# A Mamba stage whose scans carry a trailing column, with the norm root as a power, the residual summed by TensorE, fourteen products with C on GpSimd and a new order of issue

## The chip, the cores and the metric

The kernel runs on one core of one Trainium2 chip. The metric is device time in microseconds (us) of one execution. Shown are three timed executions and one that the hardware profiler recorded.

## The reference, cut to what matters

The program computes a window attention layer, a positional convolution, six Mamba layers, a gated feed-forward layer, a causal pooling and a mixture of experts over images of 2 x 256 x 56 x 56. The change touches the Mamba layers alone. There are B = 2 images of S = 3136 tokens, 512 inner channels and 16 states for each.

```python
def step(h, inp):
    u_t, dt_t, B_t, C_t = inp
    h = jnp.exp(dt_t[..., None] * A) * h + (dt_t * u_t)[..., None] * B_t[:, None, :]
    y_t = jnp.einsum('bds,bs->bd', h, C_t)
    return (h, y_t)
...
dt = jax.nn.softplus(dt_r @ dt_w + dt_b)
A = -jnp.exp(A_log)
y = selective_scan(uc, dt, A, Bm, Cm, Dp)
y = y * jax.nn.silu(z)
return y @ out_w
```

Each of the six layers works on an RMS-normed copy of the tokens, x * rsqrt(mean(x * x) + 1e-5), and adds its result to the running sum (the residual). A layernorm stands ahead of the first layer, an RMS norm behind the last.

## The kernel before, in words

`conv_phase` (attention and positions), `mamba_phase` and `tail_phase` (the rest) follow one another. `mamba_phase` cuts an image into 7 chunks of T = 448 tokens; 2 images x 6 layers x 7 chunks make 84 chunks. In a chunk the inner state has 512 x 16 rows of 448 tokens. 128 rows stand on the partitions, two such rows side by side make one step, and `order` (line 777) lists the 32 steps of a chunk: 4 blocks k of 128 channels, 4 groups ng of states, 2 pairs pr.

A step i has these parts:
- `decays(i)` (L799): two exp activations on ScalarE write exp(dt * A) for both rows into `da` (PSUM, three buffers). A first column ahead of each row comes from a BIG value in `dtr`, so that its decay is 0 there and the scan of the second row starts afresh.
- `inputs(i)` (L815, L816): ScalarE copies the two carried states into the first column of each row of `x` (SBUF, nine buffers), and GpSimd multiplies dt*u by B into the rest.
- `scan(i)` (L836): VectorE scans both rows in one instruction, h = da * h + x, and writes over `da`, or over `x` for the steps in `on_pool` (line 780, 12 of 32).
- the product with C (`times_c`, L829): on VectorE directly after the scan, or on GpSimd as `pool_product` for the steps in `on_pool`. It writes `x`.
- `keep(i)` (L825): ScalarE copies the last column of each row to `state`, for the next chunk of the same layer.
- `gather(i)` (L846, L851), for every second step: TensorE sums the products over states into `acc`. `gate(i)` (L861), for every eighth, multiplies by silu(z) on VectorE.

Beside the steps, each chunk prepares the next one: `project` (L554), the convolution (L572), `x_project`, `x_keep` (its B and C rows go through DRAM into `bc`, spread over the partitions), `dt_project`, `dt_keep`, `dt_softplus` (L636), `dt_out` (GpSimd forms dt*u, L644; dt and dt*u go to DRAM, L642, L646) and `repeat` (L773), which brings them back spread over the partitions with 8 DMAs of SP's queue a block: `dt_back` for block 0, `fetch` for the others. `y_project` (L700) and `y_add` (L707, VectorE) add the layer's result to the residual `res`. The norm ahead of a layer is `n_squares` (L654, L658), `n_root` (sqrt on ScalarE, L665), `n_invert` (reciprocal on VectorE, L668), `n_spread` (L674, TensorE) and `n_weighted` (L682, VectorE). All matmul results but `acc` pass through one PSUM buffer, `mm`.

Three tables set the order. `places` gives each preparing part its place in a chunk, counted in steps; `first` places the input layernorm's parts (in five chunks of the first layer, and in the seven of the second for the other image); `last` the final norm's. The parts of the steps stand at fixed distances from their step (lines 928 to 939). All are sorted by place (line 961) and issued in that order; each engine then works its own queue in order and waits on semaphores. `load` brings a layer's weights (L507 to L515); `w_in` has one buffer.

Of the kernel before, what the change touches and what calls it, by code (L numbers as in the profile page):

```python
# [10 lines left out]
F32 = mybir.dt.float32  # L11
# [442 lines left out]
def mamba_phase(ctx: ExitStack, tc: tile.TileContext, I, t1_d, t2_d):  # L454
# [9 lines left out]
    ctx.enter_context(tc.manual_schedule())  # L464
    T = MT
    cp = ctx.enter_context(tc.tile_pool(name="mb_const", bufs=1))
# [12 lines left out]
    nc.vector.memset(mean_w, 1.0 / C)  # L479
    eps = ones_column(nc, cp, 1e-5, "mb_eps")  # L480
    sum_w = cp.tile([P, HD], F32, name="sum_w")
    nc.sync.dma_start(sum_w, I["sum_w"])
# [4 lines left out]
    res = cp.tile([P, 2, S], F32, name="res")  # L487
    dtrs = [cp.tile([P, 4, T + 1], F32, name=f"dtr{n}") for n in range(2)]
    for t in dtrs:
        nc.gpsimd.memset(t[:, :, 0:1], BIG)  # L490

    r1_d = [dp.tile([P, 2, T], F32, name=f"r1_d{c}", bufs=1) for c in range(MCH)]

    def wide(t, n=2):
        return t.unsqueeze(1).to_broadcast([P, n, T])

# [112 lines left out]
    def x_keep(j):  # L609

        xd = M["xd"] = one.tile([DTR + 2 * DS, T], F32, name="xd")
        nc.scalar.copy(xd, M["mm"])  # L612
        bc_d = dp.tile([2 * DS, T], F32, name="bc_d")
        nc.sync.dma_start(bc_d, xd[DTR:, :])
        bc = QS[j + 1]["bc"] = two.tile([P, 8, T + 4], F32, name="bc")[:, :, 3 : T + 3]
        for n in range(4):
            nc.sync.dma_start(
                bc[chunk(n, HD)],
                bc_d.rearrange("(m n) t -> n m t", n=4)[n].unsqueeze(0).to_broadcast([HD, 8, T]),
            )  # L620
        QS[j + 1]["dt_d"], QS[j + 1]["dtu_d"] = {}, {}
# [41 lines left out]
    def root(key):  # L663
        rs = M[key] = one.tile([MTG, ng], F32, name="rs" + key)
        nc.scalar.activation(rs, M["mm"][:MTG, :ng], AF.Sqrt, bias=eps[:MTG])  # L665

    def invert(key):
        nc.vector.reciprocal(M[key], M[key])  # L668

# [26 lines left out]
    def y_project(j, k):  # L696

        ps = M["mm"] = mm()[:, :T]
        for d in range(NB):
            nc.tensor.matmul(  # L700
                ps, lhsT=layer_of(j - 1)["w_out"][:, d, chunk(k, P)],
                rhs=QS[j - 1]["hz"][:, d, :], start=(d == 0), stop=(d == NB - 1),
            )

    def y_add(j, k):
        rc = residual(j - 1)
        nc.vector.tensor_tensor(rc[:, k, :], rc[:, k, :], M["mm"], ALU.add)  # L707

# [58 lines left out]
    def repeat(Q, k):  # L767

        dtr = dtrs[k % 2]
        dtur = two.tile([P, 4, T + 4], F32, name="dtur")[:, :, 1 : T + 1]  # L770
        for t, src in ((dtr[:, :, 1:], Q["dt_d"]), (dtur, Q["dtu_d"])):
            for n in range(4):
                nc.sync.dma_start(t[chunk(n, HD)], src[k].rearrange("(g p) t -> p g t", p=HD))  # L773
        Q[k] = dtr, dtur
# [4 lines left out]

    on_pool = (2, 3, 5, 7, 8, 9, 10, 15, 19, 21, 22, 26)  # L780
    chunks = [(b, layer, c) for b in range(B) for layer in range(NL) for c in range(MCH)]
# [9 lines left out]
    def decays(i):  # L791
# [3 lines left out]
        da = pda.tile([P, 1024], F32, name="da")  # L795
        D[i] = da[:, : 2 * (T + 1)]
        for g in range(2):
            col = (4 * k + 2 * pr + g) * 4 + ng
            nc.scalar.activation(  # L799
                D[i][:, chunk(g, T + 1)], dtr[:, 2 * pr + g, :], AF.Exp,  # L800
                scale=L["am"][:, col : col + 1],
            )
# [6 lines left out]
    def inputs(i):  # L809

        j, s, k, ng, pr = at(i)
        Q = QS[j]
        X[i] = xp.tile([P, 2 * (T + 1)], F32, name="x")
        x = both(X[i])
# [8 lines left out]
    def keep(i):  # L823
        h = X[i] if i % ns in on_pool else D[i]
        nc.scalar.copy(states(i), both(h)[:, :, T : T + 1])  # L825

    def times_c(i, engine, h):
        j, s, k, ng, pr = at(i)
        engine.tensor_tensor(  # L829
            both(X[i])[:, :, 1:], both(h)[:, :, 1:], wide(QS[j]["bc"][:, 4 + ng, :]), ALU.mult  # L830
        )

    def scan(i):

        h = X[i] if i % ns in on_pool else D[i]
        nc.vector.tensor_tensor_scan(h, D[i], X[i], 0.0, ALU.mult, ALU.add)  # L836
        if i % ns not in on_pool:
            times_c(i, nc.vector, h)

    def gather(i):  # L840
# [9 lines left out]
        for g in range(4):  # L850
            nc.tensor.matmul(  # L851
                acc[0][chunk(g, HD), :T], lhsT=sum_w, rhs=both(X[i - 1 + g // 2])[:, g % 2, 1:],
                start=False, stop=(ng == 3), tile_position=(0, HD * g),
# [8 lines left out]

    def pool_product(i):
        times_c(i, nc.gpsimd, X[i])

# [17 lines left out]
    def load_rest(j):  # L883
# [5 lines left out]
    places = {  # L889
        (u_project, 0): 1.304, (u_keep, 0): 2.607, (z_project, 0): 3.501, (z_keep, 0): 3.952,  # L890
        (u_project, 1): 4.609, (u_keep, 1): 5.234, (y_project, 1): 6.869, (y_add, 1): 7.331,
        (y_project, 0): 7.461, (y_add, 0): 9.223, (u_convolve, 0): 10.048, (u_add, 0): 10.687,
        (u_project, 2): 10.964, (u_keep, 2): 11.995, (u_convolve, 1): 12.277, (u_add, 1): 13.134,
        (u_convolve, 2): 14.792, (u_add, 2): 15.184, (u_project, 3): 15.393, (u_keep, 3): 16.616,
        (u_convolve, 3): 17.440, (u_add, 3): 17.991, (z_project, 1): 18.040, (u_silu,): 18.479,
        (z_keep, 1): 18.732, (x_project,): 19.334, (x_keep,): 20.167, (dt_project, 2): 20.825,
        (dt_keep, 2): 21.601, (dt_project, 0): 21.808, (dt_keep, 0): 22.204,
        (dt_project, 1): 23.295, (dt_keep, 1): 23.374, (dt_project, 3): 24.269,
        (dt_keep, 3): 24.913, (dt_softplus,): 24.942, (dt_out, 0): 25.013, (dt_back,): 25.337,
        (z_project, 2): 25.840, (dt_out, 1): 26.057, (z_keep, 2): 26.747, (z_project, 3): 27.262,  # L900
        (load,): 27.272, (dt_out, 2): 27.694, (z_keep, 3): 28.791, (n_squares,): 29.547,
        (n_root,): 29.821, (n_invert,): 31.105, (n_spread,): 32.629, (n_weighted,): 32.761,
        (load_rest,): 34.587, (dt_out, 3): 36.194, (z_silu,): 38.909,
    }
    first = {
        f_load: 12.141, f_mean: 23.145, f_center: 23.266, f_squares: 23.712, s_root: 23.835,
        s_invert: 24.267, s_spread: 25.138, f_scale: 25.476,
    }
    last = {
        l_squares: 0.000, s_root: 0.000, s_invert: 1.571, s_spread: 2.712, l_weighted: 3.271,  # L910
        f_load: 5.288, l_out: 5.690,
    }
    n, nj = len(chunks) * ns, len(chunks)
# [13 lines left out]
    for i in range(n):  # L927
        put(i - 1.652, inputs, i)
        put(i - 1.217, decays, i)
        put(i + 0.4, scan, i)  # L930
        put(i + 1.080, keep, i)
        if i % ns in on_pool:
            put(i + 2.886, pool_product, i)
        if i % 2 == 1:
            put(i + 3.900, gather, i)
        if i % 8 == 7:
            put(i + 4.422, gate, i)
        if i % 8 == 0 and i % ns < ns - 8:
            put(i + 1.264, fetch, i)
    for j in range(-2, nj + 1):  # L940
# [559 lines left out]
```

## Time and profile before

| | us |
|---|---|
| median of three executions | 9848.73 |
| lowest and highest | 9843.43, 9856.48 |
| the profiled execution | 9833.15 |
| its span, first to last instruction | 9831.3 |

| engine | busy 0 to 600 us | busy 600 to 8520 us | busy 8520 to 9831 us |
|---|---|---|---|
| TensorE (PE) | 526.61 | 6180.35 | 1288.78 |
| VectorE (DVE) | 213.20 | 7472.47 | 703.09 |
| ScalarE (ACT) | 66.24 | 6170.21 | 521.66 |
| GpSimd (POOL) | 180.03 | 6762.92 | 177.20 |

The three stretches are about the three phases; the Mamba stage takes some 7900 of the 9831 us. A line of the groups reads: line, engine, operation, out<-in, shapes and count; then busy time in us and the mean ns of one; then the engine's idle time just before such instructions, and what ended most of it. A line of the waits reads: who waited, for whom, the total in us, how often, and the longest. In a timeline a line has its start, its length and the instruction, xN for N in a row.

### The profile page before, as it was taken

Reading aid. Unit: us, or ns where it says so; the run is one execution under the profiler, and the core shown is the slowest. Engines: PE = TensorE matmul, PEld = TensorE weight load, DVE = VectorE, ACT = ScalarE, POOL = GpSimd, SP = SyncE. Lnnn points to the kernel's source line nnn. Section 1 sums busy time; section 2 is a strip of 40 time slices with the busy share of each in tenths; the row PEclk is TensorE's granted clock in tenths of the full one; section 3 lists DMA queues with packets and bytes.
Section 4 is the critical chain, followed back from the end, with each engine's and each line's share of the span. In section 5 each row is a group of like instructions: output and inputs, shape, how many; then the busy total and the mean of one; then the engine's idle time right before and its main releaser. Section 6 shows DMA issues by size and latency. Waiting matters only on the chain. (4 is left out here: it accounts for less than half of the span.)

```text
span 9831.3 us, 102094 instructions
## 1 busy us (share of the span) xinstructions
PE 7995.7 (81%) x31026; PEld 3378.5 (34%) x31026; DVE 8388.8 (85%) x6835; ACT 6758.1 (69%) x15177; POOL 7120.1 (72%) x4860
## 2 busy tenths in 40 slices
PE   9877777777777777777777877787777777699999
PEld 6533323322222222232222222222222223255555
DVE  3338999899999999999999999999999999685453
ACT  1127777777877878777778787787877877534443
POOL 2347888788888888888898888888889888511110
PEclk9988888788888888888888888888888888799999
DMA  2235555455555555556555555555555555301111
GB/s 81 70 100 113 115 132 120 114 132 123 128 121 128 131 114 131 127 124 142 122 127 131 122 124 128 126 121 124 133 118 123 134 121 127 104 19 34 42 41 38
DMA packets 681950, 1083.41 MB, mean 110 GB/s; under 512 B 83532, under 2 KB 673169, under 8 KB 681169
## 3 DMA queue, kind: packets, MB, share of 16 engines
q1 hardware_dynamic: 681398, 1076.90, 47.1%
q8 instruction: 243, 3.98, 0.2%
q14 instruction: 309, 2.53, 0.1%
HBM read 891.71 MB, written 184.91 MB: 110 GB/s over the span
## 5 line engine op out<-in xcount | busy, mean ns | idle before, releaser
L816 POOL TENSOR_TENSOR x<-dtur,bc 128x896 f32<-128x896 f32 x2688 | 4706.5, 1775 | 109.6 <-PE acc L851 100.0
L799 ACT ACTIVATE da<-dtr,am 128x449 f32<-128x449 f32 x5376 | 3428.5, 638 | 188.1 <-DVE x L836 95.8
L836 DVE TENSOR_TENSOR_SCAN da<-da,x 128x898 f32<-128x898 f32 x1680 | 3397.1, 2022 | 144.7 <-ACT da L799 71.3
L829 POOL TENSOR_TENSOR x<-x,bc 128x896 f32<-128x896 f32 x1008 | 1791.2, 1777 | 510.6 <-ACT state L825 509.2
L554 PE MATMUL mm<-xn,w_in 128*128 128x448 f32 x2656 | 1483.3, 691 | 710.5 <-ACT hz L595 236.1
L836 DVE TENSOR_TENSOR_SCAN x<-da,x 128x898 f32<-128x898 f32 x1008 | 2001.8, 2013 | 0.7 <-ACT da L799 0.7
L829 DVE TENSOR_TENSOR x<-da,bc 128x896 f32<-128x896 f32 x1680 | 1834.4, 1092 | 80.6 <-PE mm L572 0.9
L851 PE MATMUL acc<-x,sum_w 128*32 128x448 f32 x10752 | 1565.9, 658 | 25.2 <-POOL x L829 17.7
L572 PE MATMUL mm<-u,w_cv 128*128 128x448 f32 x2656 | 1088.5, 552 | 175.5 <-ACT u L566 158.8
L554 PEld LDWEIGHTS mm<-xn,w_in 128*128 128x128 f32 x2656 | 550.3, 230 | 1684.5 <-issue 731.5
L825 ACT COPY state<-da 128x2 f32<-128x2 f32 x1680 | 264.2, 157 | 1059.4 <-DVE x L829 1041.8
L572 PEld LDWEIGHTS mm<-u,w_cv 128*128 128x128 f32 x2656 | 476.7, 189 | 801.5 <-issue 371.8
L644 POOL TENSOR_TENSOR dtu<-dt,hz 128x448 f32<-128x448 f32 x336 | 329.7, 981 | 463.4 <-ACT state L825 413.0
L700 PE MATMUL mm<-hz,w_out 128*128 128x448 f32 x1344 | 552.0, 554 | 80.2 <-DVE res L707 47.8
L625 PE MATMUL mm<-xd,w_dt 16*128 16x448 f32 x664 | 454.4, 772 | 190.7 <-ACT xd L612 111.1
L851 PEld LDWEIGHTS acc<-x,sum_w 128*32 128x32 f32 x10752 | 229.7, 117 | 1002.7 <-issue 792.2
L815 ACT COPY x<-state 128x2 f32<-128x2 f32 x2688 | 521.7, 194 | 0.0
L1348 DVE TENSOR_TENSOR hid<-hid,cb 128x784 f32<-128x784 f32 x128 | 135.2, 1057 | 423.8 <-ACT hid L1345 400.4
L799 ACT ACT_TABLE_LOAD x346 | 443.9, 1283 | 7.0 <-DMA dtr<-dt_d 1.0
L658 PE MATMUL mm<-mb_mean_w,sq 128*112 128x1 f32 x1744 | 259.5, 279 | 231.0 <-ACT sq L654 230.2
L846 PE MATMUL acc<-hz,w_sk 128*128 128x448 f32 x672 | 369.4, 635 | 63.1 <-DVE hz L861 61.8
L700 PEld LDWEIGHTS mm<-hz,w_out 128*128 128x128 f32 x1344 | 242.5, 190 | 403.7 <-issue 191.2
(217 smaller groups left out, 8949.1 us busy)
## 6 DMA issues: line engine op xcount, KB each, us to landing
dtr<-dt_d SPq DMA_DIRECT2D x1344, 224.0 KB
dtur<-dtu_d SPq DMA_DIRECT2D x1344, 224.0 KB
bc<-bc_d SPq DMA_DIRECT2D x336, 448.0 KB
dt_d<-dt SPq DMA_DIRECT2D x336, 224.0 KB
dtu_d<-dtu SPq DMA_DIRECT2D x336, 224.0 KB
cb<-comb_d SPq DMA_DIRECT2D x128, 196.0 KB
t<-t_d SPq DMA_DIRECT2D x28, 448.0 KB
w_in<-in_in_w SPq DMA_DIRECT2D x12, 1024.0 KB
```

Of the source, the lines that this page charges most:

```text
L554: nc.tensor.matmul(ps, lhsT=layer_of(j + 1)["w_in"][:, k, chunk(at, P)], rhs=Q["xn"][:, k, :], start=(k == 0), stop=(k == 1),)
L572: nc.tensor.matmul(ps, lhsT=layer_of(j + 1)["w_cv"][:, 4 * d + k, :], rhs=M["u", d][:, k : k + T], start=(k == 0), stop=(k == 3),)
L625: nc.tensor.matmul(ps, lhsT=layer_of(j + 1)["w_dt"][:, chunk(d, P)], rhs=M["xd"][:DTR, :], start=True, stop=True,)
L644: nc.gpsimd.tensor_tensor(dtu, dt[:, d, :], hz(j)[:, d, :], ALU.mult)
L700: nc.tensor.matmul(ps, lhsT=layer_of(j - 1)["w_out"][:, d, chunk(k, P)], rhs=QS[j - 1]["hz"][:, d, :], start=(d == 0), stop=(d == NB - 1),)
L799: nc.scalar.activation(D[i][:, chunk(g, T + 1)], dtr[:, 2 * pr + g, :], AF.Exp, scale=L["am"][:, col : col + 1],)
L815: nc.scalar.copy(x[:, :, 0:1], states(i))
L816: nc.gpsimd.tensor_tensor(x[:, :, 1:], Q[k][1][:, 2 * pr : 2 * pr + 2, :], wide(Q["bc"][:, ng, :]), ALU.mult)
L829: engine.tensor_tensor(both(X[i])[:, :, 1:], both(h)[:, :, 1:], wide(QS[j]["bc"][:, 4 + ng, :]), ALU.mult)
L836: nc.vector.tensor_tensor_scan(h, D[i], X[i], 0.0, ALU.mult, ALU.add)
L846: nc.tensor.matmul(acc[0][:, :T], lhsT=L["w_sk"][:, k, :], rhs=Q["hz"][:, k, :], start=True, stop=False,)
L851: nc.tensor.matmul(acc[0][chunk(g, HD), :T], lhsT=sum_w, rhs=both(X[i - 1 + g // 2])[:, g % 2, 1:], start=False, stop=(ng == 3), tile_posi ...
```

## The change

- Each row gets one more column at its end (R = 450 for 449): `dtr` is 0 there (decay exp(0) = 1), `dtur` and `bc` are 0 (input 0), so the scan repeats the end state in it. `keep` reads that column; the products with C leave it alone. The tiles `dtur` and `bc` become two fixed buffers each, zeroed once in the column.
- `root` adds 1e-5 with Identity for Sqrt on ScalarE; `invert` becomes a power of -0.5 on GpSimd.
- `y_project` adds the residual by one more matmul with the identity; `y_keep` (ScalarE) copies the sum back to `res`.
- `on_pool` has 14 steps, and other ones. The product is its own event, `product`, for both engines.
- `places` has new values; `inputs`, `decays`, `product`, `keep`, `gather` and `gate` get a table with a place of their own for each step of a chunk (`scan` stays at 0.4); `fetch` moves from 1.264 to 3.407; some parts of `first` and `last` move up to the part ahead of them.

```diff
-    T = MT
+    T, R = MT, MT + 2
...
+    half = ones_column(nc, cp, -0.5, "half")
...
-    dtrs = [cp.tile([P, 4, T + 1], F32, name=f"dtr{n}") for n in range(2)]
-    for t in dtrs:
-        nc.gpsimd.memset(t[:, :, 0:1], BIG)
+    dtrs = [cp.tile([P, 4, R], F32, name=f"dtr{n}") for n in range(2)]
+    dturs = [cp.tile([P, 4, T + 4], F32, name=f"dtur{n}")[:, :, 1:R] for n in range(2)]
+    bcs = [cp.tile([P, 8, T + 4], F32, name=f"bc{n}")[:, :, 3:] for n in range(2)]
+    for n in range(2):
+        nc.gpsimd.memset(dtrs[n][:, :, 0:1], BIG)
+        nc.gpsimd.memset(dtrs[n][:, :, R - 1 :], 0.0)
+        nc.gpsimd.memset(dturs[n][:, :, T:], 0.0)
+        nc.gpsimd.memset(bcs[n][:, :, T:], 0.0)
...
-        nc.scalar.activation(rs, M["mm"][:MTG, :ng], AF.Sqrt, bias=eps[:MTG])
+        nc.scalar.activation(rs, M["mm"][:MTG, :ng], AF.Identity, bias=eps[:MTG])
 
     def invert(key):
-        nc.vector.reciprocal(M[key], M[key])
+        nc.gpsimd.tensor_tensor(
+            M[key], M[key], half[:MTG].to_broadcast([MTG, ng]), ALU.pow
+        )
...
-                rhs=QS[j - 1]["hz"][:, d, :], start=(d == 0), stop=(d == NB - 1),
-            )
-
-    def y_add(j, k):
-        rc = residual(j - 1)
-        nc.vector.tensor_tensor(rc[:, k, :], rc[:, k, :], M["mm"], ALU.add)
+                rhs=QS[j - 1]["hz"][:, d, :], start=(d == 0), stop=False,
+            )
+        nc.tensor.matmul(ps, lhsT=ident, rhs=residual(j - 1)[:, k, :], start=False, stop=True)
+
+    def y_keep(j, k):
+        nc.scalar.copy(residual(j - 1)[:, k, :], M["mm"])
...
-    on_pool = (2, 3, 5, 7, 8, 9, 10, 15, 19, 21, 22, 26)
+    on_pool = (0, 2, 3, 4, 7, 9, 12, 15, 16, 17, 19, 24, 26, 31)
...
-        nc.scalar.copy(states(i), both(h)[:, :, T : T + 1])
+        nc.scalar.copy(states(i), both(h)[:, :, R - 1 :])
 
     def times_c(i, engine, h):
         j, s, k, ng, pr = at(i)
         engine.tensor_tensor(
-            both(X[i])[:, :, 1:], both(h)[:, :, 1:], wide(QS[j]["bc"][:, 4 + ng, :]), ALU.mult
+            both(X[i])[:, :, 1 : R - 1], both(h)[:, :, 1 : R - 1],
+            wide(QS[j]["bc"][:, 4 + ng, :T]), ALU.mult,
...
-        if i % ns not in on_pool:
-            times_c(i, nc.vector, h)
...
-    def pool_product(i):
-        times_c(i, nc.gpsimd, X[i])
+    def product(i):
+        if i % ns in on_pool:
+            times_c(i, nc.gpsimd, X[i])
+        else:
+            times_c(i, nc.vector, D[i])
...
-        (dt_keep, 3): 24.913, (dt_softplus,): 24.942, (dt_out, 0): 25.013, (dt_back,): 25.337,
-        (z_project, 2): 25.840, (dt_out, 1): 26.057, (z_keep, 2): 26.747, (z_project, 3): 27.262,
-        (load,): 27.272, (dt_out, 2): 27.694, (z_keep, 3): 28.791, (n_squares,): 29.547,
-        (n_root,): 29.821, (n_invert,): 31.105, (n_spread,): 32.629, (n_weighted,): 32.761,
-        (load_rest,): 34.587, (dt_out, 3): 36.194, (z_silu,): 38.909,
+        (dt_keep, 1): 26.336, (dt_softplus,): 26.771, (dt_out, 0): 27.197, (z_project, 2): 27.256,
+        (dt_out, 1): 27.383, (z_keep, 2): 27.659, (load,): 28.502, (z_project, 3): 28.731,
+        (dt_back,): 28.792, (dt_out, 2): 29.162, (dt_out, 3): 29.351, (z_keep, 3): 29.771,
+        (n_squares,): 29.916, (n_root,): 30.842, (n_invert,): 31.013, (n_spread,): 31.087,
+        (n_weighted,): 31.687, (load_rest,): 34.722, (z_silu,): 38.072,
...
+        f_load: 12.141, f_mean: 23.145, f_center: 23.148, f_squares: 23.822, s_root: 23.825,
+        s_invert: 24.267, s_spread: 25.138, f_scale: 25.141,
...
+    steps = {
+        inputs: (
+            -1.10, -3.56, -2.02, -1.43, -1.68, -2.58, -2.72, -0.88, -0.74, -1.72, -1.99, -1.68, -2.65,
+            -1.28, -3.64, -2.90, -0.57, -2.57, -2.05, -1.06, -2.03, -2.58, -1.99, -1.91, -3.10, -1.71,
+            -1.17, -4.25, -3.92, -0.42, -5.08, -2.98,
+        ),
...
+        product: (
+            1.59, 1.40, 4.74, 2.23, 2.85, 1.45, 0.40, 1.16, 1.40, 2.29, 1.40, 0.40, 2.79, 0.40, 1.45,
+            1.68, 2.19, 2.81, 0.45, 4.18, 0.45, 1.40, 0.40, 0.40, 0.87, 0.40, 2.92, 1.40, 0.45, 1.45,
+            0.45, 2.10,
+        ),
...
+        keep: (
+            1.36, 2.00, 3.09, 3.53, 1.93, 1.39, 1.88, 1.36, 0.64, 4.97, 1.99, 1.03, 2.26, 1.61, 1.36,
+            1.49, 3.53, 2.94, 1.85, 4.34, 0.41, 1.66, 0.42, 0.92, 2.47, 2.10, 3.59, 2.10, 2.02, 2.38,
+            1.46, 1.70,
+        ),
...
-        put(i - 1.652, inputs, i)
-        put(i - 1.217, decays, i)
         put(i + 0.4, scan, i)
-        put(i + 1.080, keep, i)
-        if i % ns in on_pool:
-            put(i + 2.886, pool_product, i)
-        if i % 2 == 1:
-            put(i + 3.900, gather, i)
-        if i % 8 == 7:
-            put(i + 4.422, gate, i)
+        for what, place in steps.items():
+            every = ns // len(place)
+            if i % every == every - 1:
+                put(i + place[i % ns // every], what, i)
         if i % 8 == 0 and i % ns < ns - 8:
-            put(i + 1.264, fetch, i)
+            put(i + 3.407, fetch, i)
```

## The prediction

> **What bounds the kernel now.** I read the page's busy table first, then the busy time in 100 us windows, then the groups of lines and the waits of the Mamba stage, and last the timeline of VectorE through one chunk.
>
> ```profile
> PE 7995.7 (81%) x31026; PEld 3378.5 (34%) x31026; DVE 8388.8 (85%) x6835; ACT 6758.1 (69%) x15177; POOL 7120.1 (72%) x4860
> 5500.00:5600.00 100.00, 79.14 (x289) 28.43 (x287) 98.13 (x69) 80.62 (x188) 89.38 (x55) 0.88 0.55 121
> ```
>
> After the stretch and its length, the columns of a window are PE, PEld, DVE, ACT, POOL, clock, DMA share, GB/s. The averages of the first line hide the stage: in the Mamba stage (about 700 to 8480 us, 84 chunks) VectorE is busy 97 to 98% of an ordinary window, GpSimd 88 to 90%, ScalarE and TensorE near 79%. VectorE sets the pace. Windows with the side job of input normalisation fall to 89 to 92%.
>
> The groups of VectorE and GpSimd over the page:
>
> ```profile
> L816 POOL TENSOR_TENSOR x<-dtur,bc 128x896 f32<-128x896 f32 x2688 | 4706.5, 1775 | 109.6 <-PE acc L851 100.0
> L836 DVE TENSOR_TENSOR_SCAN da<-da,x 128x898 f32<-128x898 f32 x1680 | 3397.1, 2022 | 144.7 <-ACT da L799 71.3
> L829 POOL TENSOR_TENSOR x<-x,bc 128x896 f32<-128x896 f32 x1008 | 1791.2, 1777 | 510.6 <-ACT state L825 509.2
> L829 DVE TENSOR_TENSOR x<-da,bc 128x896 f32<-128x896 f32 x1680 | 1834.4, 1092 | 80.6 <-PE mm L572 0.9
> L799 ACT ACT_TABLE_LOAD x346 | 443.9, 1283 | 7.0 <-DMA dtr<-dt_d 1.0
> L665 ACT ACT_TABLE_LOAD x109 | 139.8, 1283 | 1.9
> L707 DVE TENSOR_TENSOR res<-res,mm 128x448 f32<-128x448 f32 x168 | 101.3, 603 | 7.7 <-PE mm L700 7.7
> ```
>
> A chunk has 32 scans; 20 products with C are on VectorE, 12 on GpSimd. The timeline of VectorE gives what each costs in place, start to start; "x2" is two in a row:
>
> ```profile
> 5509.68 0.61 DVE L861 TENSOR_TENSOR hz<-hz,acc 128x448 f32<-128x448 f32 x1
> 5510.21 2.03 DVE L836 TENSOR_TENSOR_SCAN da<-da,x 128x898 f32<-128x898 f32 x1
> 5512.27 1.09 DVE L829 TENSOR_TENSOR x<-da,bc 128x896 f32<-128x896 f32 x1
> 5513.28 2.03 DVE L836 TENSOR_TENSOR_SCAN da<-da,x 128x898 f32<-128x898 f32 x1
> ...
> 5592.30 0.60 DVE L707 TENSOR_TENSOR res<-res,mm 128x448 f32<-128x448 f32 x1
> 5592.81 3.94 DVE L836 TENSOR_TENSOR_SCAN x<-da,x 128x898 f32<-128x898 f32 x2
> ...
> 5599.72 0.61 DVE L861 TENSOR_TENSOR hz<-hz,acc 128x448 f32<-128x448 f32 x1
> ```
>
> The same gate comes back after 5599.72 - 5509.68 = 90.0 us: one ordinary chunk. Scan to scan with a product between is 3.07 us, scan to scan without is 1.94 (the second of "3.94 x2" starts some 1.93 later), so a product costs 1.13, of which 0.12 is the gap of a product that waits for the scan just ahead of it. A residual sum costs 0.51.
>
> SP's timeline in the same chunk, behind the first dtu product (it ended at 5550.28):
>
> ```profile
> 5550.31 0.34 SPq L646 DMA_DIRECT2D dtu_d<-dtu  x1
> 5551.27 1.74 SPq L773 DMA_DIRECT2D dtr<-dt_d  x4
> 5553.11 1.81 SPq L773 DMA_DIRECT2D dtur<-dtu_d  x4
> ```
>
> Eight DMAs of 224 KB are 1.8 MB. In windows of 1 us the queue moves 176 to 269 GB/s from 5552 to 5561, so dtur has landed near 5561: 10.7 us after that product ended.
>
> The waits of the Mamba stage show where GpSimd's slack of 10 us a chunk goes and what VectorE still waits for:
>
> ```profile
> POOL x L829 <- ACT state L825: 509.2, 228, 3.8
> POOL dtu L644 <- ACT state L825: 413.0, 82, 14.1
> ACT state L825 <- DVE x L829: 1028.4, 730, 2.7
> DVE da L836 <- ACT da L799: 71.3, 83, 0.9
> DVE rss L668 <- ACT rss L665: 39.0, 12, 3.9
> ```
>
> **What the Trainium skill says.** "ScalarE: Activation LUTs", What ACT_TABLE_LOAD costs: a load takes about 1283 ns; the trace has 1283 in all. Its section Table sets says that cheap functions such as identity are in every set, sqrt has its own: so root as Identity needs no load. "VectorE: DVE Perf Modes", The TRN2 errata, gives (N+151)/0.96 ns for an fp32 tensor_tensor: 1091 for N=896, and the trace shows 1092 with one operand in PSUM. "GPSIMD Engine Reference", Key points: GpSimd shares its SBUF interfaces with VectorE and contends with instructions that have two SBUF inputs. Scan, product, gate and residual sum each have one input in PSUM, and the GpSimd product keeps within 1760 to 1807 ns, so moving products shouldn't stretch them. No page prices a power on GpSimd.
>
> **Part by part, for one ordinary chunk.**
>
> Products 12 to 14 on GpSimd. VectorE: 2 x 1.13 = 2.3 us less. GpSimd: 2 x 1.74 more (five inputs in a row took 8.69).
>
> The product is no longer queued with its scan. In the order as built, 14 of the 18 that stay still follow their own scan directly and 4 don't: 4 x 0.12 = 0.5 less.
>
> Residual sum by TensorE. VectorE: 2 x 0.51 = 1.0 less. TensorE: two more fp32 products with the identity, 552.0/672 = 0.82 us each, 1.6 a chunk, hidden in an engine 79% busy. ScalarE: two copies of 0.52 (row of L595). While a copy waits for PE, decays queue behind it; before, scans did.
>
> Norm root. ScalarE loses 1.25 sqrt loads a chunk (105 in the stage) and as many exp reloads: 2.5 x 1.28 = 3.2 us against the 1.0 just added, so it falls from 72 to about 70 us of 90. VectorE loses a reciprocal (0.09), and 39.0 us in all of waiting for rss. GpSimd gets a power of 112x4. No row shows one. Low end 0.2 us (a GpSimd copy of 128x6 took 205 ns). High end: 448 values one by one, each at ten times the 1.98 ns a column of L816, 9 us. I take 0.5, four columns in the ordinary way at ten times that price over a fixed part near 0.4.
>
> Trailing column. Each scan gets two elements: 32 x 2 x 2.25 ns = 0.14 us more on VectorE; GpSimd's inputs are 449 wide: 32 x 2 x 1.98 ns = 0.13 more; decays the same in ScalarE's slack. In return the end state is outside what the product overwrites: in the built order the GpSimd products wait for the scan alone. That frees the 509.2 us. The copy itself waited for the product (1028.4 us); now eight end-state copies a chunk are placed behind a GpSimd product and wait for it. Queued behind each on ScalarE are decays, which the scans need. ScalarE's spare 20 us should cover them: nothing, or up to 1.7 us each (a product's length) if the cover fails.
>
> New order, SP. Fetch moves in the list from 1.264 to 3.407 steps behind the block's start; its 8 DMAs pass no other DMA of an ordinary chunk, and SP waits there for buffers to come free anyway: nothing. dt_back, with 8 DMAs, moves from 25.337 to 28.792, so the two DMAs of dt_out 1 (0.34 us each) now stand ahead of it: it lands some 11.5 us after the first dtu product. What hid those DMAs on GpSimd was, in the order of before, two dtu, five inputs and a product ahead of the next chunk's first input: 2 x 0.94 + 6 x 1.735 = 12.3 us. In the new one (dt_out 3 comes forward too, input 1 of the next chunk is 3.56 steps early) there are dtu, two inputs, a product, two dtu: 3 x 0.94 + 3 x 1.735 = 8.0. So GpSimd is short of work for 3.5 us, and all next inputs queue behind. Bounds: 0, if it has been late for other reasons, and 5, if the transfers share the engines. I take 3.5.
>
> Where a layer changes (11 times), the five weight loads of load stood behind dt_back (27.272 against 25.337) and now stand ahead of it (28.502 against 28.792): w_in must wait there for the last z_project of the old layer, and its 1 MB with 0.5 of w_out takes some 7 us at the rate above. VectorE has inputs in hand for part of that; I take 5 us each, 55, bounds 0 and 12.
>
> New order, norm. Root to weighting is 0.85 steps (2.4 us), was 2.94 (8.3). The chain needs root 0.26, power 0.5, the rest of a product on GpSimd 0.9, spreading 170.1/83 = 2.05: 3.7. VectorE may wait 1.3 us, scans behind it; bounds 0 and 3. I take 1.0, since ScalarE can run ahead.
>
> Sum on VectorE: 90.0 - 2.3 - 0.5 - 1.0 - 0.1 + 0.14 = 86.2, with the new wait 87.2. On GpSimd: 46 x 1.735 + 4 x 0.94 + 0.13 + 0.5 = 84.2 of work, with 3.5 of waiting 87.7. So what is late next is GpSimd, and a chunk gains 2.3; 84 x 2.3 = 193. The rss waits give 39 more; against them, f_scale now stands directly behind its spread and may wait 1.5 us in 12 chunks, 18; and the 55. Total 159. The profiled execution took 9833.15 us (span 9831.3): 9674. It lies 16 below the median 9848.73, so I forecast 9690.
>
> **Rivals.**
> - More gain: GpSimd isn't short of work, because X buffers or scans had held it back before. For: its 10 us of slack vanish into work. Against: the DMAs' 11 us are in the trace. VectorE sets the pace at 86.6, layer changes at half price: 84 x 3.4 + 21 - 28 = 279, 9570.
> - Slower: GpSimd waits twice in one chain, for the softplus (untouched: 413.0 us over 84 chunks, 3.35 in the chunk shown) and then for dtur. 84.2 + 3.4 + 3.5 + 1.2 (acc) = 92.3: 84 x 2.3 - 21 + 55 = 227 more, 10076. It decides from waits of 90.0 - 84.2 = 5.8 us a chunk. Against: a GpSimd without slack reaches dtu later and finds the softplus done. A power at its high end would come to the same side.
> - Half of that second wait stays, or some of the eight copies delay decays: 89.2, 84 x 0.8 + 21 - 55 = 33, 9816.
> - It doesn't do what it says: the new order's waits eat all that leaves VectorE: about 9849.
>
> **Numbers.** Chances: forecast 0.43 (own range 9620 to 9760), more gain 0.27 (9480 to 9620), half the wait 0.10 (9760 to 9829), nothing left 0.05, slower 0.15 (most by the double wait). The range 9510 to 9840 leaves out the slower case and the ends, about 2 in 10. About 0.2% (20 us) is what a measurement can tell from no change: faster 0.80, same 0.05, slower 0.15.
>
> **What would show it.** Right: ordinary windows with GpSimd at 95% and VectorE at 95%; 1176 products on GpSimd; no load on the root's line and 105 fewer on the decays'; no wait of GpSimd products for end states; GpSimd waiting some 3.5 us a chunk for dtur, weighting about 1. Wrong: no wait for dtur (more gain); dtu still waiting 3 us beside it (slower); a power above 2 us; VectorE waiting for da (the copies); GpSimd products above 1.85 us.

## The result and the profile after

The changed kernel ("after" in what follows) takes 10589.02 us (median of four runs, 10587.34 to 10598.01) against 9846.08 beside it (9830.73 to 9856.48): 1.0758 times the time of before, 95% interval 1.0739 to 1.0776. It is 743 us slower, where 159 less had been forecast.

The busy line of the page after, and then its window of the same 100 us as shown of before:

```profile
PE 8053.7 (76%) x31362; PEld 3458.3 (33%) x31362; DVE 8110.4 (77%) x6388; ACT 6581.8 (62%) x15131; POOL 7725.7 (73%) x5146
```

```profile
5500.00:5600.00 100.00, 71.22 (x268) 26.92 (x264) 86.95 (x58) 71.06 (x170) 89.09 (x53) 0.86 0.52 116
```

VectorE has lost 278 us of work (8388.8 to 8110.4), about as planned. But its share of the window fell from 98 to 87%, GpSimd's stayed at 89%, and no engine is above 90%: the loss is in waits, not in work. An ordinary chunk (gate to gate, 5508.90 to 5607.05) is 98.15 us where it was 90.0. In it VectorE works 85.1 us and waits 12.3; GpSimd works 87.2 and waits 10.9.

The waits of the page after (who, for whom, total us, times, longest):

```profile
DVE xn L690 <- PE mm L682: 671.2, 83, 24.4
DVE x L836 <- ACT state L832: 203.3, 168, 3.1
DVE da L844 <- ACT da L806: 150.1, 154, 2.0
POOL x L823 <- PE acc L857: 442.3, 88, 9.3
POOL x L823 <- DMA dt_d<-dt: 183.9, 41, 7.9
POOL x L823 <- DMA dtur<-dtu_d: 180.6, 19, 16.2
POOL x L823 <- DMA dtu_d<-dtu: 52.9, 9, 14.7
ACT state L832 <- DVE x L836: 721.8, 387, 4.7
ACT state L832 <- DVE x L844: 642.2, 156, 10.0
```

GpSimd's wait for end states (509.2) is gone, as forecast, and so are the 109 sqrt loads (of the exp reloads 95 went where 105 were forecast). New is VectorE's wait at the weighting: 671.2/84 = 8.0 us a chunk. GpSimd's wait for `acc`, at the matmuls of the gather, grew from 100.0 us to 442.3 (5.3 a chunk), and the three DMA rows make 417.4 us. Two of the signs of being wrong that the prediction named show as well: VectorE waits for decays (150.1 and 114.2 us), and a product on GpSimd is longer than 1.85 us. Two groups of GpSimd:

```profile
L836 POOL TENSOR_TENSOR x<-x,bc 128x896 f32<-128x896 f32 x1176 | 2269.0, 1932 | 121.4 <-DVE x L844 115.5
L674 POOL TENSOR_TENSOR rsn<-rsn,half 112x4 f32<-112x4 f32 x84 | 85.0, 1012 | 1.3 <-ACT rsn L671 1.3
```

A product on GpSimd takes 1932 ns where it took 1777, and the power 1.01 us. How the waits hang together is seen in one chunk, on ScalarE, GpSimd and VectorE in turn:

```profile
5518.06 0.62 ACT L637 ACTIVATE dt<-mm,vec 128x448 f32<-128x448 f32 x1
5522.87 0.23 ACT L832 COPY state<-da 128x2 f32<-128x2 f32 x2 [4.18 <-DVE x L836]
5522.98 0.21 ACT L822 COPY x<-state 128x2 f32<-128x2 f32 x1
5523.07 0.65 ACT L637 ACTIVATE dt<-mm,vec 128x448 f32<-128x448 f32 x1
...
5544.30 0.26 ACT L671 ACTIVATE rsn<-mm,mb_eps 112x4 f32<-112x4 f32 x1 [0.43 <-PE mm L664]
```

```profile
5542.16 1.92 POOL L650 TENSOR_TENSOR dtu<-dt,hz 128x448 f32<-128x448 f32 x2
5549.19 3.51 POOL L823 TENSOR_TENSOR x<-dtur,bc 128x898 f32<-128x898 f32 x2 [5.11 <-DMA dtu_d<-dtu]
5552.66 1.01 POOL L674 TENSOR_TENSOR rsn<-rsn,half 112x4 f32<-112x4 f32 x1
```

```profile
5546.50 2.02 DVE L844 TENSOR_TENSOR_SCAN x<-da,x 128x900 f32<-128x900 f32 x1
5555.80 1.27 DVE L690 SCALAR_TENSOR_TENSOR xn<-res,vec,mm 128x448 f32<-128x448 f32 x2 [7.28 <-PE mm L682]
```

ScalarE stands 4.18 us at an end-state copy that waits for a product, and the second `dt_keep` stands behind that copy. The input waits 5.11 us for the DMAs of dt*u. ScalarE's part of the root (L671) is ready at 5544.56, but the power is queued behind two inputs that wait for those DMAs and starts 8.1 us later. Weighting waits for the power, and VectorE's scans stand behind weighting. These are three queues worked in order, each with one instruction that isn't ready ahead of ones that are. Whether the 4.18 us reached the power by way of `dt_keep` isn't shown.

### The profile page after: what moved, and what is told of

Same layout as the page of the kernel before. It is cut to its first block, busy times and chain, and to the rows that moved or that the text cites. A ratio compares the mean times of both kernels' runs of the same rounds, so it can differ in the third digit from the quotient of the medians.

```text
span 10585.6 us, 101621 instructions
## 1 busy us (share of the span) xinstructions
PE 8053.7 (76%) x31362; PEld 3458.3 (33%) x31362; DVE 8110.4 (77%) x6388; ACT 6581.8 (62%) x15131; POOL 7725.7 (73%) x5146
## 5 line engine op out<-in xcount | busy, mean ns | idle before, releaser
L823 POOL TENSOR_TENSOR x<-dtur,bc 128x898 f32<-128x898 f32 x2688 | 4724.1, 1780 | 921.5 <-PE acc L857 442.3
L806 ACT ACTIVATE da<-dtr,am 128x450 f32<-128x450 f32 x5376 | 3390.0, 637 | 222.7 <-DMA dtr<-dt_d 62.1
L844 DVE TENSOR_TENSOR_SCAN da<-da,x 128x900 f32<-128x900 f32 x1512 | 3054.9, 2026 | 188.6 <-ACT da L806 150.1
L844 DVE TENSOR_TENSOR_SCAN x<-da,x 128x900 f32<-128x900 f32 x1176 | 2365.8, 2020 | 117.9 <-ACT da L806 114.2
L836 POOL TENSOR_TENSOR x<-x,bc 128x896 f32<-128x896 f32 x1176 | 2269.0, 1932 | 121.4 <-DVE x L844 115.5
L836 DVE TENSOR_TENSOR x<-da,bc 128x896 f32<-128x896 f32 x1512 | 1637.9, 1088 | 264.0 <-ACT state L832 203.3
L857 PE MATMUL acc<-x,sum_w 128*32 128x448 f32 x10752 | 1497.8, 650 | 40.9 <-POOL x L836 36.3
L682 PE MATMUL mm<-mb_ident,rsn 112*128 112x112 f32 x664 | 170.0, 438 | 693.1 <-POOL rsn L674 693.1
L708 PE MATMUL mm<-hz,w_out 128*128 128x448 f32 x1344 | 552.1, 554 | 114.2 <-ACT res L715 113.4
L690 DVE SCALAR_TENSOR_TENSOR xn<-res,vec,mm 128x448 f32<-128x448 f32 x166 | 105.6, 677 | 671.2 <-PE mm L682 671.2
L832 ACT COPY state<-x 128x2 f32<-128x2 f32 x1176 | 210.7, 190 | 642.2 <-DVE x L844 642.2
```

Source lines behind the costliest of these rows:

```text
L708: nc.tensor.matmul(ps, lhsT=layer_of(j - 1)["w_out"][:, d, chunk(k, P)], rhs=QS[j - 1]["hz"][:, d, :], start=(d == 0), stop=False,)
L806: nc.scalar.activation(D[i][:, chunk(g, R)], dtr[:, 2 * pr + g, :], AF.Exp, scale=L["am"][:, col : col + 1],)
L823: nc.gpsimd.tensor_tensor(x[:, :, 1:], Q[k][1][:, 2 * pr : 2 * pr + 2, :], wide(Q["bc"][:, ng, :]), ALU.mult)
L832: nc.scalar.copy(states(i), both(h)[:, :, R - 1 :])
L836: engine.tensor_tensor(both(X[i])[:, :, 1 : R - 1], both(h)[:, :, 1 : R - 1], wide(QS[j]["bc"][:, 4 + ng, :T]), ALU.mult,)
L857: nc.tensor.matmul(acc[0][chunk(g, HD), :T], lhsT=sum_w, rhs=both(X[i - 1 + g // 2])[:, g % 2, 1 : R - 1], start=False, stop=(ng == 3), ti ...
```

## The experiments

Times are medians of four runs or more; ratios are to the kernel before on the same chip, with 95% intervals.

**One wait of the new order at a time.** Squares, root and power 2.1 to 2.3 steps earlier (the expectations below say three); these are the entries that change:

```diff
-        (n_squares,): 29.916, (n_root,): 30.842, (n_invert,): 31.013
+        (n_squares,): 27.700, (n_root,): 28.700, (n_invert,): 28.710
```

> The changed kernel with squares, root and power of the next norm moved ahead of the next chunk's first inputs in the list (27.700, 28.700, 28.710); spread and weighting stay. Queue theory (VectorE is held at the weighting because the power stands in GpSimd's queue behind inputs that wait for the DRAM round trip of dt): the weighting's wait of 671 us falls under 100 us, and the time falls by up to 671, to about 9920. Late-data theory (the round trip ends late anyway and the scans need those inputs): the weighting's wait goes too, but scans then wait for x; in the chunk looked at, the inputs were done 4.3 us before the weighting ended, so 84 x 4.3 = 360 less, 10230. Work theory (GpSimd simply has too much to do): under 100 less, about 10500.

Measured: 10511.33, 1.0692 (1.0666 to 1.0718), 78 less than after. The weighting wait is gone, and VectorE waits elsewhere. Its waits:

```profile
DVE da L844 <- ACT da L806: 390.9, 316, 2.4
DVE x L844 <- ACT da L806: 231.9, 112, 4.9
DVE x L836 <- ACT state L832: 231.7, 168, 3.1
DVE x L844 <- POOL x L823: 172.5, 13, 15.7
```

The dt chain at about its places of before, again by the entries that change:

```diff
-        (dt_project, 1): 26.189, (dt_keep, 1): 26.336, (dt_softplus,): 26.771, (dt_out, 0): 27.197
-        (dt_out, 1): 27.383, (dt_back,): 28.792
+        (dt_project, 1): 24.300, (dt_keep, 1): 24.900, (dt_softplus,): 24.942, (dt_out, 0): 25.013
+        (dt_out, 1): 26.057, (dt_back,): 25.337
```

> The changed kernel with the last dt product, softplus, dt_out 0, dt_out 1 and dt_back at the places they had before (24.300 and 24.900 for dt_project 1 and dt_keep 1, then 24.942, 25.013, 26.057, 25.337). Late-data and queue theory alike: GpSimd's waits for dt_d, dtu_d and dtur (417 us) and the weighting's 671 us both fall under 100 us; about 9850 to 9950. Work theory: GpSimd has 87 us of work a chunk and still stalls elsewhere, the waits move to x from the product's gather; above 10300.

Measured: 10476.53, 1.0660 (1.0638 to 1.0682), 112 less. The inputs' wait for DMAs is gone and the weighting wait falls to 214.2; scans wait 491.1 for decays instead, and 352.9 on GpSimd moved to `dtu`, whose buffers the earlier DMAs hold.

Root by Sqrt on ScalarE and reciprocal on VectorE again, all else as after:

```diff
-        nc.scalar.activation(rs, M["mm"][:MTG, :ng], AF.Identity, bias=eps[:MTG])
+        nc.scalar.activation(rs, M["mm"][:MTG, :ng], AF.Sqrt, bias=eps[:MTG])
...
-        nc.gpsimd.tensor_tensor(
-            M[key], M[key], half[:MTG].to_broadcast([MTG, ng]), ALU.pow
-        )
+        nc.vector.reciprocal(M[key], M[key])
```

> The changed kernel with the norm root as before: Sqrt on ScalarE, reciprocal on VectorE at the power's place in the list. Queue theory: the weighting no longer waits for GpSimd; its wait falls from 671 to about 100 us, ScalarE gets 105 sqrt loads and as many exp reloads back (270 us, mostly in its slack); about 9950 to 10050. Late-data theory: as with the power moved, about 10230. Work theory: only the power's 1.0 us is saved, 112 us, about 10480.

Measured: 10403.22, 1.0586 (1.0564 to 1.0607), 186 less. The weighting wait falls to 58.5. GpSimd's waits for `acc` (470) and DMAs (about 422) stay.

The moves of the first two at once:

> The changed kernel with both moves made before one at a time: squares, root and power three steps earlier, and the dt chain (dt_project, softplus, dt_out, dt_back) at the places of before. Alone they gave 78 and 112 us. If the waits are independent terms, 190 us: 10400. If each only uncovers the next queue's wait (the theory now), about the larger of the two, 10440 to 10500.

Measured: 10555.64, 1.0728 (1.0707 to 1.0749): 33 less than after, less than either alone. Neither expectation had that. Now the power itself waits, 311.4 us until an end-state copy of ScalarE is done and 237.9 until a DMA is, and scans wait 587.7 for decays. The waits aren't terms of a sum. The medians of this group and of after come from different chips (the kernel before took 9823.52 to 9839.62 us on the group's and 9846.08 beside after). By the ratios the four kernels gain 65, 96, 169 and 30 us, each to some 30 us either way, so that the two moves together are hardly clear of no gain.

The first two results are those that the theory of too much work on GpSimd had expected. The run with 14 steps in the old order, further below, speaks against that theory.

**The parts without the order.** The changed kernel with the whole order of before (places, distances, 12 steps on GpSimd), so with column, power and residual by TensorE:

> The changed kernel with the whole order of before: its places, fixed distances and its twelve steps on GpSimd; the trailing column, the power and the residual on TensorE stay. Order theory (the new order puts instructions that others wait for behind waits in in-order queues; the parts themselves are harmless): VectorE loses two residual sums a chunk (1.0 us) and the reciprocal's wait, about 9846 - 86 - 39 = 9720, up to 9800. Parts theory (the slower GpSimd product, the power in GpSimd's queue or the copies on ScalarE cost it): above 10200, most of the 743 us stays.

Measured: 9890.07, 1.0056 (1.0039 to 1.0074), between the two expectations. The order, with its choice of 14 steps, carries 699 of the 743 us. Then each part alone in the kernel before, by the lines of the change's diff that belong to it: the column (`R`, `dtrs`, `dturs`, `bcs`, `keep`, `times_c`),

> The kernel before with the trailing column alone (order, sqrt, reciprocal, residual sum on VectorE as before). Is the longer GpSimd product (1932 against 1777 ns) the column's? If it is, 1932 here too: 12 x 0.155 = 1.9 us more on GpSimd a chunk, inside its slack of 10; the 509 us that products waited for end states go. Order theory: within 30 us of before, 9815 to 9860. Parts theory: slower by 100 us or more.

9883.82, 1.0049 (1.0034 to 1.0065), again between the two expectations: the 509.2 us of waiting for end states go, but each of the 1008 products on GpSimd is 160 ns longer, 161 us, and inputs wait 312.3 for `acc`, products 139.3 for scans. The power,

> The kernel before with the norm root as a power on GpSimd alone. Order theory: in the old order 1.5 steps lie between power and spread, so 1.0 us on GpSimd is in its slack, the weighting waits under 1 us a chunk, the sqrt loads go: 9760 to 9830. Queue theory at its strictest (a power in GpSimd's queue is always late): VectorE's wait at the weighting is 3 us a chunk or more, 10000 or more.

9841.49, 1.0009 (1.0000 to 1.0017): no difference that can be told, where a gain had been expected, for a power of 1 us on GpSimd. And the residual (the matmul with the identity is added as in the change):

```diff
-        nc.vector.tensor_tensor(rc[:, k, :], rc[:, k, :], M["mm"], ALU.add)
+        nc.scalar.copy(rc[:, k, :], M["mm"])
```

> The kernel before with the residual summed by TensorE and copied back by ScalarE, at the places of the sums on VectorE. Order theory: VectorE loses 2 x 0.51 us a chunk, 86 less, about 9760. Rival: the copies make ScalarE late for the decays and mm is held longer, no gain, 9846 or more.

9890.61, 1.0052 (1.0033 to 1.0071). VectorE's work falls by 80 us as reckoned (8388.8 to 8309.2), and the time rises by 60. Three waits of that kernel grew, and the same three in the kernel before:

```profile
DVE da L837 <- ACT state L826: 113.7, 60, 2.6
DVE x L837 <- ACT da L800: 85.0, 75, 1.2
ACT hz L584 <- PE mm L572: 374.2, 328, 2.0
```

```profile
DVE da L836 <- ACT state L825: 66.3, 46, 2.6
DVE x L836 <- ACT da L799: 0.7, 1, 0.7
ACT hz L584 <- PE mm L572: 104.1, 166, 0.8
```

I read it so: the extra matmuls and copies lengthen the chain through the one buffer `mm`, ScalarE waits there, and decays behind it are late. That isn't shown: whether the matmuls or the copies do it was not tried apart.

**The order taken apart.** Three kernels: the order of before with the 14 steps; the new places with the distances and 12 steps of before; the new distances and 14 steps with the places of before:

> The changed kernel with the whole order of before (places and step distances), but with the 14 steps of on_pool kept; column, power and residual by TensorE kept as well. Beside the run with the order of before and 12 steps (9890), it is the choice of 14 steps alone. Theory (the order's places cost the time, the 14 products do not): VectorE loses 2 x 1.1 us a chunk and GpSimd gains 2 x 1.94, so GpSimd's work is about 32 x 1.78 + 14 x 1.94 + 4 x 0.94 + 1 = 89 us a chunk against 90: within 9800 to 10000. Rival (14 longer products overload GpSimd, and the order is only where this shows): GpSimd becomes the bound with its waits on top, 5 us and more a chunk: 10300 or above.

> The changed kernel with the new places of the preparing parts (and of the first and last norm), but the step distances, fetch and the 12 steps of on_pool of before. Theory A (the late chain dt_project, softplus, dt_out, dt_back, root, power, weighting of the preparing parts costs most): 10300 to 10550. Theory B (the distances of the steps themselves, end-state copies and gathers standing ahead of what they hold up, cost most): 9900 to 10050.

> The changed kernel with its new step distances, fetch and 14 steps of on_pool, but the places of before for the preparing parts (and for the first and last norm). Theory A (the late chain of the preparing parts costs most): 9900 to 10050. Theory B (the distances of the steps cost most): 10300 to 10550. If both this run and the one with the new places alone stay well under 10589, the two tables' waits come from their standing together; if both are near 10500, either alone uncovers the same slack.

| places | distances | steps on GpSimd | us | ratio to before |
|---|---|---|---|---|
| before | before | 12 | 9890.07 | 1.0056 (1.0039 to 1.0074) |
| before | before | 14 | 9982.76 | 1.0152 (1.0127 to 1.0177) |
| before | new | 14 | 10589.24 | 1.0762 (1.0741 to 1.0784) |
| new | before | 12 | 10890.41 | 1.1075 (1.1050 to 1.1099) |
| new | new | 14 | 10589.02 | 1.0758 (1.0739 to 1.0776) |

The 14 steps (two more, and of the 12 of before only seven are among them) cost 93 us even in the old order. The busy line of that kernel:

```profile
PE 8184.1 (82%) x31362; PEld 3442.4 (34%) x31362; DVE 8147.1 (82%) x6388; ACT 6576.2 (66%) x15131; POOL 7711.0 (77%) x5146
```

GpSimd has as much work in it as in after (7711.0 us against 7725.7), and it is 606 us faster. So too much work on GpSimd isn't what the new order costs. The new distances alone cost as much as the whole new order, the new places alone more; both lie above every range given for them. So neither table is the innocent one, and no share can be given to either.

In the fourth row, with the two moves of the first group made:

> The new places with the step distances of before (10890), and in it the two moves: squares, root and power three steps earlier, and the dt chain at the places of before. Theory (in the new places the chain dt_project to weighting stands too late in a chunk, and nothing else in them is short): the 523 us of the weighting wait and GpSimd's wait for dtur go, 10100 to 10300. Rival (the other new places, those of the projections, convolutions and sums in the first two thirds of a chunk, hold mm or acc up as well): above 10450.

10404.97, 1.0582 (1.0567 to 1.0598), between the two expectations: 485 less than the fourth row. The late chain is about half of what the new places cost with the old distances; 515 us stay, with waits of GpSimd for `acc` (503.2) and for the softplus (407.0, where the fourth row has 426.7).

In the third row, end-state copies no later than before; gathers no later than before; and inputs, copies and gathers together:

```diff
-        keep: (1.36, 2.00, 3.09, 3.53, 1.93, ...
+        keep: (1.08, 1.08, 1.08, 1.08, 1.08, ...
...
-        gather: (3.45, 4.29, 2.81, 2.72, 6.32, 5.31, 4.80, ...
+        gather: (3.45, 3.90, 2.81, 2.72, 5.10, 3.90, 3.90, ...
...
-        inputs: (-1.10, -3.56, -2.02, ...
+        inputs: (-1.652,) * 32,
```

> The new step distances with the places of before (10589), and in it every end-state copy no later than 1.08 steps behind its step, as before (new distances below that stay). Theory (end-state copies placed behind products make ScalarE wait, and decays and the VectorE products behind them are late): the 472 us that VectorE's products wait for end-state copies go, and 200 to 470 us of the time with them: 10120 to 10390. Rival (another queue's head-of-line wait takes its place, as with the moves of the power and of the dt chain): 10480 to 10600.

> The new step distances with the places of before (10589), and in it the gathers no later than 3.9 steps behind their step, as before (three bound otherwise: step 9 at 5.1, step 19 at 4.62; earlier ones stay). Theory (GpSimd's inputs wait for buffers of x that the late gathers hold, 649 us): most of that wait goes and 200 us or more of the time: below 10390. Rival (another wait takes its place, or the gathers were late because TensorE stood at mm): 10480 to 10600.

> The new step distances with the places of before (10589), with three tables put back at once: inputs at -1.652 for every step, end-state copies at most 1.08 and gathers at most 3.9 (5.1 and 4.62 for steps 9 and 19). What stays new: decays, products, gates, fetch and the 14 steps. The order of before with the 14 steps took 9983. If the waits come from these three tables together: 9980 to 10200. If the decays' and products' own distances carry them: 10400 or above.

In this order: 11091.26, 1.1281 (1.1262 to 1.1299); 10535.38, 1.0716 (1.0700 to 1.0732); 11257.07, 1.1447 (1.1430 to 1.1464). With the gathers earlier, GpSimd's wait for `acc` falls from 649.2 to 363.1 us, while its wait for ScalarE's copies into `x` rises from 111.5 to 300.1: 54 us gained. My theory that late copies are the fault falls: early ones cost 502 us, and with inputs and gathers put back as well the kernel is slower still, 668 us behind the third row. In the kernel with early copies, VectorE's wait for them and a piece of its timeline:

```profile
DVE x L836 <- ACT state L832: 645.0, 570, 6.3
```

```profile
5533.10 2.01 DVE L844 TENSOR_TENSOR_SCAN da<-da,x 128x900 f32<-128x900 f32 x1
5535.88 1.09 DVE L836 TENSOR_TENSOR x<-da,bc 128x896 f32<-128x896 f32 x1 [0.77 <-ACT state L832]
```

The product and the copy both only read `da`, yet in this program the second in the list waits for the first. After has four VectorE steps whose copy comes first. In two of them the product waits (step 8, 0.64 against 1.40; step 20, 0.41 against 0.45): 168 = 2 x 84 waits. In steps 5 and 14, where copy and product lie within 0.1 of a step, none shows. With copies at 1.08 there are nine such steps, and 570 such waits. The copies in turn stand on ScalarE behind decays and behind copies that wait for matmuls. So I took it that a copy, its product and the next decays must be placed together. The test of that puts decays, copies and VectorE's products back as one:

```diff
-        decays: (0.21, -0.39, ...
+        decays: (-1.217,) * 32,
...
+        keep: (1.080,) * 32,
```

and 0.4 for the 18 products on VectorE; inputs, GpSimd's products, gathers, gates and fetch stay new.

> The new step distances with the places of before (10589), and in it ScalarE's and VectorE's tables put back together: decays at -1.217, products of the 18 VectorE steps at 0.4 (directly behind their scan), end-state copies at 1.08, behind those products again. What stays new: inputs, GpSimd's products, gathers, gates, fetch and the 14 steps. All of it put back took 9983. Theory now (the end-state copies alone put the copies ahead of products that then wait for them, and late decays stand behind copies that wait for scans; the two engines' queues have to be put back together): VectorE's waits for end states and decays fall from 960 us to below 200, and the time to 9980 to 10150. Rival (GpSimd's inputs behind buffers that late gathers and products hold are the bound): 10350 or above.

10179.46, 1.0340 (1.0324 to 1.0355): 410 of the 606 us between rows two and three of the table. What is left on ScalarE's account, and GpSimd's wait for `acc`:

```profile
DVE da L844 <- ACT state L832: 136.1, 85, 2.0
DVE da L844 <- ACT da L806: 73.0, 72, 3.0
DVE x L844 <- ACT state L832: 58.4, 52, 2.5
POOL x L823 <- PE acc L857: 443.9, 130, 5.2
```

In the kernel of the third row VectorE's waits were:

```profile
DVE x L836 <- ACT state L832: 472.4, 168, 6.4
DVE x L844 <- ACT da L806: 314.7, 112, 4.6
DVE da L844 <- ACT da L806: 172.3, 127, 2.4
```

So VectorE waits 267 us for end states and decays where it waited 960, and no product of its own waits for a copy any more; I had expected under 200, and the time 30 us lower. Decays or products put back alone were not tried. The other 197 us belong to the inputs, GpSimd's products, gathers, gates and fetch; which of these was not taken apart.

**The longer product.** In after, `x` shifted by one element, so that rows start one element later:

> The changed kernel with the x rows shifted by one element in SBUF (tile of 2R+2, used from column 1), to see whether the 155 ns by which the GpSimd product became slower (1932 against 1777) hang on where its rows start. If they do: 1777 again, 14 x 0.155 = 2.2 us a chunk less on GpSimd. Queue and late-data theory: most of it lies ahead of the same wait, 0 to 60 us less, 10530 to 10590. Work theory: all of it, 185 less, 10400. If the start does not matter: 1932 and 10589.

11804.04, 1.2010 (1.1986 to 1.2034), and the product still 1932 ns: an offset of one element isn't it. (The time, far above what was expected, says nothing of the product: in this program inputs also wait for ScalarE's copies into `x`, 786.5 us. Why was not looked into.) In the column-only kernel, two trailing columns:

```diff
-    T, R = MT, MT + 2
+    T, R = MT, MT + 3
```

> The kernel before with the trailing column alone (9884), but two such columns in each row instead of one (rows of 451, products still 448 wide; rows of bc one element longer). It asks why a GpSimd product takes 1937 ns with one trailing column and 1777 without. If the evenness of the row's length is the cause (450 against 449): 1777 ns again. If the gap of more than one element between the two rows is: 1937 ns or more. If the product's own length of 448 in a longer tile isn't it and bc's rows are: the inputs change too. Time 9870 to 9900 either way (GpSimd isn't the bound there), or up to 20 less.

9896.09, 1.0050 (1.0033 to 1.0067). GpSimd's groups in it, and then in the kernel with one column:

```profile
L821 POOL TENSOR_TENSOR x<-dtur,bc 128x900 f32<-128x900 f32 x2688 | 5169.9, 1951 | 92.1 <-PE acc L855 83.4 <-DMA dtur<-dtu_d 8.5
L834 POOL TENSOR_TENSOR x<-x,bc 128x896 f32<-128x896 f32 x1008 | 1985.0, 1969 | 0.0
```

```profile
L821 POOL TENSOR_TENSOR x<-dtur,bc 128x898 f32<-128x898 f32 x2688 | 4729.8, 1784 | 321.1 <-PE acc L855 312.3 <-DMA dtur<-dtu_d 8.5 <-issue 0.2
L834 POOL TENSOR_TENSOR x<-x,bc 128x896 f32<-128x896 f32 x1008 | 1952.4, 1937 | 162.2 <-DVE x L842 139.3 <-PE acc L855 22.8
```

The product stays long with odd rows, so evenness isn't the cause. A gap of more than one element between rows would fit the products but not the inputs, which got longer with a gap of one. The column with its new tiles is the cause (it alone brings the longer product, in the old order); what in it, the rows' length or where the tiles lie, is open. No kernel here beats the one before; the power alone equals it within what can be told.

## Why the prediction was wrong

The sum on VectorE's own work held (86.2 forecast with its gaps; 98.15 less the 12.3 of waits is 85.9). What failed are steps that priced waits, above all those of the new order: the forecast gave it 1.0 us of waiting a chunk on VectorE, nothing on ScalarE and 3.5 on GpSimd. In after VectorE waits 12.3 in an ordinary chunk and GpSimd 10.9, and the order carries 699 of the 743 us. Two steps that priced work failed as well.

- **"New order, norm": "VectorE may wait 1.3 us ... I take 1.0", bound 3.** Measured 8.0. The step that failed: it counted "the rest of a product on GpSimd" ahead of the power, but not that the inputs in the same queue, found two paragraphs earlier to wait for DMAs, stand ahead of it. The two waits were costed apart and are one behind the other. Moving the root off GpSimd took 186 us; moving the power took the wait but only 78, because VectorE then waited elsewhere.
- **"ScalarE's spare 20 us should cover them: nothing".** Spare time doesn't cover an engine that stands at the head of its queue. ScalarE's waits at end-state copies are 1364 us in the two rows, 16 a chunk (1041.8 and 12 before), and what stood behind was not only decays but `dt_keep`, the start of the chain to the power. Nor does it go the way that the prediction feared: no end-state copy waits for a GpSimd product in after, all such waits end with VectorE's products and scans. Putting decays, copies and VectorE's products back gave 410 us (with the places of before). The four products that no longer follow their scan were booked as a gain of 0.5, with nothing for the copies placed before or behind them.
- **"So GpSimd is short of work for 3.5 us".** About right: without the layer changes the DMA waits are 262 us in 73 chunks, 3.6 each. The 11 longest, one at each layer change, add 155.3 us, 14.1 each; against an ordinary chunk's 3.6 that is 116 in all where I took 55, inside its bounds. But this wait wasn't the only one on GpSimd: `acc` adds 5.3 a chunk where only the slower rival counted 1.2.
- **"The GpSimd product keeps within 1760 to 1807 ns, so moving products shouldn't stretch them."** The prediction looked for a stretch from VectorE; it was the column, costed at 0.27 us, that stretched them: 14 x 0.155 = 2.2 us a chunk. With the power at 1.01 for 0.5, GpSimd's work is 87.2 for 84.2, so that even without a wait no more than about 2.8 of the 90.0 could have been won.
- **"Residual sum ... hidden in an engine 79% busy".** In the kernel before with this part alone VectorE's 1.0 a chunk went, and the time rose by 60 us: 144 worse than the gain of 84 forecast. That it came through `mm` and ScalarE is my reading.
- **"The rss waits give 39 more":** the power alone gave no gain.

The slower rival had the right side and not the mechanism: GpSimd's wait for the softplus shrank, as the argument against it said, and the second wait was `acc`. The rival's point (5.8 us of waits a chunk on GpSimd) was passed at 10.9.

## What to carry to other kernels

When an order is changed, write for each engine the queue around the moved instruction and ask at each place what stands behind one that isn't ready; "spare time" on that engine was no cover here. The waits of this order didn't add: taking one away uncovered another (78 and 112 us apart, 33 together), and the places of a copy, its product and the next decays paid only when moved together. Before work is taken off the pacing engine, look for a single buffer in the chain that it is moved to; here the residual sum cost 60 us, and I take such a buffer for the reason.

## What the runs showed of the hardware

- A GpSimd product of two rows of 448 takes 1777 ns in rows of 449, 1929 to 1944 in rows of 450 (means of the kernels here) and 1969 in rows of 451. The input product takes 1771 to 1775 with 448 columns in rows of 449, 1778 to 1791 with 449 in rows of 450, and 1951 with 450 in rows of 451. Within one kernel the product with C is steady (1910 to 1978 over the 1176 of after), though VectorE works beside it.
- A power of 112x4 on GpSimd takes 1.01 us, twice the 0.5 that I took and far from the 9 of the upper bound.
